# Four tail stages per chunk in place of three in the short blocks of a sparse attention kernel

## The chip, the cores and the metric

The kernel runs on one core of one Trainium2 chip. The metric is device time in microseconds for one launch. The time before is the median of three runs; the profile is of one further execution, whose own time is given beside it.

## What is computed

The input is a batch of 8 graphs with 2048 nodes and 128 features each, all with the same adjacency matrix, in which a node has some 16 neighbours on average (each entry is set with a chance of 0.0078). Four layers follow one another. Layers 0 and 1 are masked attention with 8 heads of 16, a residual, a normalisation, a feed-forward part of width 256 and a second normalisation; layers 2 and 3 are graph attention with a residual and a normalisation:

```
# layers 0 and 1
scores = einsum(Q, K) / sqrt(16);  scores = where(adj == 0, -inf, scores)
x = layer_norm(h + (softmax(scores) @ V) @ Wo + bo)
x = layer_norm(x + relu(x @ W1 + b1) @ W2 + b2)
# layers 2 and 3
h = x @ W;  e = leaky_relu(h @ a_src [i] + h @ a_dst [j]), masked by adj
x = layer_norm(softmax(e) @ h + x)
```

## The kernel before

The kernel works on the neighbours alone. It sorts the nodes by their number of neighbours and cuts them into 16 blocks of 128 (one node per partition). Block t has CAPS[t] neighbour slots: 29, 23, 21, 20, 19, 18, 17, 17, 16, 15, 15, 14, 13, 13, 12, 10. For every layer a table in memory holds one row per node (keys and values of all 8 graphs in layers 0 and 1, 8 KB), and a slot is filled by a GpSimd gather of 128 rows (`gather`, issued at L321).

A **chunk** is two slots in layers 0 and 1 and four in layers 2 and 3, so a block of 16 or 15 slots has eight chunks, one of 14 or 13 has seven, one of 12 six and one of 10 five. In `attention_chunk` VectorE multiplies keys by queries (L657) and adds halves (L663); TensorE turns the result by eight transposes and so sums it to scores (L335 into `pair`), to which masks are added (L672); ScalarE takes the exponential (L679); TensorE turns it back (L683); ScalarE copies it out as the weights (L687); VectorE multiplies the values by them (L695); TensorE sums values into `acc` by sixteen transposes (L335 into `acc`, in two halves). At the end of a block, and once in between when it has seven chunks or more, `block_sums` adds up the weights (L636, L641, L646).

When a block's last chunk is weighed, `sums` adds the two halves of the sum (L708), `scales` makes the reciprocal and turns it (L710, L730, L335 into `m`, L741), and `tail` (the function of this name) waits four slots, scales the result (`outputs`, L723) and starts the two halves of `attention_tail`, one slot and four slots later. A half tail covers four of the eight graphs: residual and Wo (L754, L759, L763), normalisation (L502, L492, L493, L509), transposes (L342), scaling (L513), two W1 products (L776) with ReLU (L781), the W2 group (L788, L793), the second normalisation, transposes, and the projection to the next layer's rows (L539, with copies L545 or L549). Each `yield` in it ends a **stage**; there are about sixteen in a half. When both halves are through, `state_done` sends the rows to the next layer's table (`put_rows`, L526).

The order of all this is written out by the kernel itself: `layers` goes over all chunks of all layers and, three times per chunk, calls `slot`. A slot advances every generator in `threads` by one step and every one in `tails` by one stage, and issues gathers (`fetch`) up to four chunks ahead, in seven buffers. It advances the tails a second time where the current chunk's layer still waits for the table of the layer before, and, in every third slot, where `hurry()` is true. `hurry()` is true only for chunks of layers 2 and 3. The engines then take their instructions in that order. Within a chunk, the second slot stands behind the scores, and the third behind the first half of the sum of the chunk two before.

The first two blocks of layers 1 to 3 can begin before the table is whole: their lists are sorted so that early slots need only the rows of earlier blocks; the rest waits for the last rows.

Of the kernel before, what the change touches and what calls it, by code (L numbers as in the profile page):

```python
# [33 lines left out]
RING = 9  # L34
STATES = 4
SCALED = 1

# [2 lines left out]
CAPS = [BASE + FOLD, 23, 21, 20, 19, 18, 17, 17, 16, 15, 15, 14, 13, 13, 12, 10]  # L42
# [47 lines left out]
def sparse_path(ctx: ExitStack, tc: tile.TileContext, ins: dict, out: bass.AP, flag: bass.AP):  # L90
# [718 lines left out]
    def gat_chunk(l, c):  # L809
# [18 lines left out]
        if c["folded"]:  # L828
            box["wf"] = small.tile([P, FOLD, NB], F32, tag="wf", name="wf", bufs=1)
            nc.vector.tensor_max(box["wf"], wa, wb)  # L830
        ws = small.tile([P, 4, SCALED], F32, tag="ws", name="ws", bufs=3)
        nc.vector.tensor_max(  # L832
            ws[:, :ns, :], wa[:, :, NB - SCALED :], wb[:, :, NB - SCALED :]
        )
        yield
        hv = hs[:, :, : NB * D].rearrange("p s (b c) -> p s b c", b=NB)
        nv = NB - SCALED
        nc.vector.tensor_mul(  # L838
# [330 lines left out]
    for l in range(4):  # L1169
        per = 2 if l < 2 else 4  # L1170
        for t, k, ns, folded in pieces(l, per):
            c = dict(l=l, t=t, k=k, ns=ns, folded=folded, box=blocks[l][t])
# [33 lines left out]
    def hurry():  # L1206

        c = every[min(now[0], len(every) - 1)]
        return c["l"] == 2 and c["t"] == NT - 1 or c["l"] > 1 and put[c["l"]] < NT

    def slot():
        advance(threads)
        advance(tails)
        fetch()
        beat[0] += 1
        c = every[min(now[0], len(every) - 1)]
        if c["l"] > 0 and put[c["l"]] < NT or beat[0] % 3 == 0 and hurry():
            advance(tails)
# [642 lines left out]
```

## Time and profile before

| what | value |
|---|---|
| median of three runs | 2790.73 us (2790.14 to 2792.69) |
| the profiled execution | 2798.62 us, of which its span 2796.7 |
| mean granted TensorE clock | 0.939 |
| block ends in layer 0 (L708), blocks 7, 13 and 15 | 681.0, 969.8, 1041.2 us |
| block ends in layer 1 (L708), blocks 7, 13 and 15 | 1556.7, 1821.9, 1887.4 us |
| last table write (L526) for layer 1, for layer 2 | 1104.3, 1949.3 us |

All times within the profile count from the span's start. Engines are named PE (TensorE products), PEld (its weight loads), DVE (VectorE), ACT (ScalarE), POOL (GpSimd) and SP (SyncE). A line of the profile's groups gives the kernel's line, the engine and operation, what is written and read, how often, the busy time and the mean length of one in ns, and then the engine's idle time just before these instructions with what ended it. A line of the timeline gives start, length, engine, line and, in brackets, the idle time before it.

### The profile page before, as it was taken

To read this page: it belongs to the slowest core of one execution; us is meant where nothing else is said; L and a number is where in the kernel's file an instruction comes from. 1 tells how busy PE (TensorE), PEld (TensorE's weight loads), DVE (VectorE), ACT (ScalarE), POOL (GpSimd) and SP (SyncE) were. 2 spreads that over 40 slices of the span, in tenths; PEclk is the share of its full clock that TensorE was granted. 3 is DMA by queue.
4 is the path that set the end of the run, shared out by engine and by line. 5 is a ranking of instruction groups with operands and counts; after the bars stand their busy time and mean duration, and the time that the engine had idled before them with its cause. 6 is when DMAs were issued, how large, how long until landed. Compare 5 with 4: busy or idle time off the path is not lost.

```text
span 2796.7 us, 48901 instructions
## 1 busy us (share of the span) xinstructions
PE 2345.7 (84%) x17811; PEld 2126.5 (76%) x17811; DVE 2513.7 (90%) x2467; ACT 1381.6 (49%) x5032; POOL 1755.3 (63%) x1346
## 2 busy tenths in 40 slices
PE   5866889898899998798989999997677887878885
PEld 4655788787788887688878888886567776878885
DVE  9698999999899897999999999986889997799995
ACT  3611444454455665154445556566346566355554
POOL 3367788678656454545565566562776776677772
PEclk9978999999999999999999999999789888999997
DMA  9898999999999888789999999984999998999994
GB/s 365 275 373 311 369 349 345 376 338 350 369 337 355 336 320 315 306 320 369 348 390 369 354 374 368 349 328 172 367 412 413 375 367 326 347 411 413 406 402 157
DMA packets 195426, 973.64 MB, mean 348 GB/s; under 512 B 30012, under 2 KB 31804, under 8 KB 123184
## 3 DMA queue, kind: packets, MB, share of 16 engines
q0 software_dynamic: 172080, 885.06, 82.5%
q1 hardware_dynamic: 18346, 60.00, 5.5%
q10 hardware_dynamic: 4752, 25.36, 2.7%
q8 instruction: 144, 2.36, 0.3%
q14 instruction: 104, 0.85, 0.1%
HBM read 917.09 MB, written 87.36 MB: 359 GB/s over the span
## 4 chain that ended last, share of the span: by engine, by line
PE 42%; DVE 24%; DMA 16%; issue 8%; ACT 8%; POOL 1%; ACTq 0%; POOLq 0%; DVEq 0%; SPq 0%
PE acc L335 15%; DMA kv<-table,lists 9%; DVE kv L695 8%; DVE kv L657 8%; PE pair L335 4%; PE m L793 4%; PE m L776 3%; PE m L539 3%; PE m L342 2%; DVE kv L838 2%; PE m L788 2%; PE m L593 2%; PE m L759 2%; PE m L763 2%; DMA table<-rows,perm 2%
## 5 line engine op out<-in xcount | busy, mean ns | idle before, releaser
L321 POOL DMA_INDIRECT kv<-table,lists x938 | 1282.2, 1367 | 678.0 <-PE acc L335 269.8
L335 PE MATMUL acc<-ident,kv 128*128 128x128 f32 x8048 | 1052.9, 285 | 159.6 <-DVE kv L695 87.9
L335 PEld LDWEIGHTS acc<-ident,kv 128*128 128x128 f32 x8048 | 957.6, 148 | 222.4 <-DVE kv L695 111.1
L695 DVE TENSOR_TENSOR kv<-kv,weights 128x2048 f32<-128x2048 f32 (+1 forms) x282 | 625.8, 2219 | 25.9 <-ACT weights L687 25.8
L657 DVE TENSOR_TENSOR kv<-kv,q 128x2048 f32<-128x2048 f32 (+1 forms) x280 | 618.2, 2208 | 32.0 <-DMA kv<-table,lists 26.3
L838 DVE TENSOR_TENSOR kv<-kv,pair 128x3584 f32<-128x3584 f32 (+1 forms) x150 | 530.8, 3538 | 1.0
L335 PE MATMUL pair<-ident,kv 128*128 128x128 f32 (+1 forms) x2256 | 301.3, 277 | 86.1 <-issue 72.8
L663 DVE TENSOR_TENSOR kv<-kv 128x1024 f32<-128x1024 f32 (+1 forms) x282 | 334.8, 1187 | 9.2
L335 PEld LDWEIGHTS pair<-ident,kv 128*128 128x128 f32 (+1 forms) x2256 | 257.0, 141 | 106.4 <-issue 85.1
L321 POOL DMA_INDIRECT kv<-table,sorted_lists x150 | 192.8, 1286 | 139.7 <-PE acc L335 42.9
L679 ACT ACTIVATE ring<-pair 128x128 f32<-128x128 f32 (+1 forms) x282 | 77.8, 276 | 365.0 <-PE pair L335 292.9
L502 ACT ACTIVATE n<-m,eps 128x128 f32<-128x128 f32 x512 | 181.5, 371 | 137.6 <-PE m L793 133.3
L687 ACT COPY weights<-pair 128x128 f32<-128x128 f32 (+1 forms) x282 | 73.3, 260 | 350.9 <-PE pair L683 342.7
L843 ACT ACTIVATE kv<-kv,ws 128x128 f32<-128x128 f32 x544 | 174.5, 398 | 145.0 <-DVE ws L832 136.4
L793 PE MATMUL m<-w_L,hT 128*128 128x128 f32 x1024 | 157.3, 276 | 0.0
L509 ACT ACTIVATE n<-m,rs 128x128 f32<-128x128 f32 x512 | 146.4, 376 | 0.3
L793 PEld LDWEIGHTS m<-w_L,hT 128*128 128x128 f32 x1024 | 136.1, 193 | 0.0
L776 PE MATMUL m<-n1T,w_L 128*128 128x512 f32 x256 | 132.9, 604 | 3.0 <-ACT hT L781 1.8
L723 DVE TENSOR_TENSOR o<-acc,scale 128x512 f32<-128x512 f32 x128 | 83.3, 684 | 52.0 <-ACT scale L741 27.1
L526 POOL DMA_INDIRECT table<-rows,perm x57 | 82.1, 1441 | 70.1 <-ACT own L562 18.7
L342 PE MATMUL m<-ident,n 128*128 128x128 f32 x640 | 114.9, 293 | 11.9 <-ACT n L509 5.6
L342 PEld LDWEIGHTS m<-ident,n 128*128 128x128 f32 x640 | 79.6, 145 | 51.0 <-ACT n L509 23.3
(254 smaller groups left out, 3614.2 us busy)
## 6 DMA issues: line engine op xcount, KB each, us to landing
kept<-xT SPq DMA_DIRECT2D x40, 512.0 KB, 6.7
kv<-in_adj_dram SPq DMA_DIRECT2D x16, 1024.0 KB, 15.6
table<-kv ACTq DMA_DIRECT2D x16, 1024.0 KB, 4.5
xT<-kept SPq DMA_DIRECT2D x32, 512.0 KB, 8.0
kv<-table,lists POOLq DMA_INDIRECT x938, 8.6
kv<-in_x_nodes_dram ACTq DMA_DIRECT2D x16, 512.0 KB, 9.9
kv<-table,sorted_lists POOLq DMA_INDIRECT x150, 6.9
home<-kept SPq DMA_DIRECT2D x4, 512.0 KB, 15.3
```

What stands on the lines that cost most here:

```text
L321: this = nc.gpsimd.indirect_dma_start(out=dst, out_offset=None, in_=tables[l][:, :] if need == NT else views[l][0], in_offset=bass.Indirec ...
L335: nc.tensor.matmul(dst, src, ident, start=start, stop=True, is_transpose=True, skip_group_check=True)
L342: nc.tensor.transpose(pt[:, j * P : (j + 1) * P], src[:, j, :], ident)
L502: nc.scalar.activation(dst[:, i, :], z[:, i, :], AF.Square, bias=eps, scale=D**-0.5, accum_out=ss[:, i : i + 1],)
L509: nc.scalar.mul(dst[:, i, :], z[:, i, :], rs[:, i : i + 1])
L657: nc.vector.tensor_mul(kk, kk, q[:, None].to_broadcast([P, ns, NB, D]))
L663: nc.vector.tensor_add(hk.rearrange("p j (c h) -> p c j h", h=NH), kj[:, :, :NH, :], kj[:, :, NH:, :])
L695: nc.vector.tensor_mul(vv, vv, w.rearrange("p (s b h) -> p (s b) h", b=NB, h=NH)[:, :, None, :] .to_broadcast([P, ns * NB, HD, NH]),)
L776: nc.tensor.matmul(ph, wt["1"][:, f * P : (f + 1) * P], n1T.rearrange("p b c -> p (b c)"), start=True, stop=True,)
L793: nc.tensor.matmul(y[:, j, :], hT[:, f, j, :], wt["2"][:, f, :], start=False, stop=f == 1, skip_group_check=True,)
L838: nc.vector.tensor_mul(hv[:, :, :nv, :], hv[:, :, :nv, :], wc[:, :, :nv, None].to_broadcast([P, ns, nv, D]))
L843: nc.scalar.mul(hv[:, i, b, :], hv[:, i, b, :], ws[:, i, b - nv : b - nv + 1])
```

## The change

A constant is added, and `hurry()` answers for layers 0 and 1 too: it is true when the current chunk belongs to a block of at most sixteen slots, that is to blocks 8 to 15. In those, one slot in three advances the tails by two stages. The chunks themselves, `threads` and the gathers keep their places.

```diff
+SHORT = 16
...
     def hurry():
         c = every[min(now[0], len(every) - 1)]
+        if c["l"] < 2:
+            return CAPS[c["t"]] <= SHORT
         return c["l"] == 2 and c["t"] == NT - 1 or c["l"] > 1 and put[c["l"]] < NT

     def slot():
         advance(threads)
         advance(tails)
         fetch()
         beat[0] += 1
         c = every[min(now[0], len(every) - 1)]
         if c["l"] > 0 and put[c["l"]] < NT or beat[0] % 3 == 0 and hurry():
             advance(tails)
```

## The prediction

> **What bounds the kernel now.** I read the page first: no engine is at its limit over the whole span, VectorE comes nearest, and TensorE follows.
>
> ```profile
> PE 2345.7 (84%) x17811; PEld 2126.5 (76%) x17811; DVE 2513.7 (90%) x2467; ACT 1381.6 (49%) x5032; POOL 1755.3 (63%) x1346
> ...
> PE 42%; DVE 24%; DMA 16%; issue 8%; ACT 8%; POOL 1%; ACTq 0%; POOLq 0%; DVEq 0%; SPq 0%
> ```
>
> The second line is the chain that ended last: TensorE holds 42% of it, VectorE 24%. An average hides the stages, so I asked for the busy time of the four stretches that the edit can touch: layer 0's blocks from the end of 8, the turn from layer 0 to 1, layer 1's blocks from 9, and the turn to layer 2. The columns are length, then busy time of PE, PEld, DVE, ACT and POOL, the clock, the DMA share and GB/s.
>
> ```profile
> 739.00:1041.00 302.00, 288.05 (x2219) 258.00 (x2218) 277.73 (x206) 171.47 (x584) 168.78 (x106) 0.98 0.91 347
> 1041.00:1105.00 64.00, 58.75 (x418) 49.31 (x417) 44.01 (x27) 41.72 (x144) 24.96 (x16) 1.00 0.76 276
> 1605.00:1887.00 282.00, 268.65 (x2169) 242.73 (x2168) 263.70 (x160) 163.77 (x623) 171.66 (x104) 0.99 0.93 354
> 1887.00:1970.00 83.00, 57.96 (x413) 49.66 (x412) 47.30 (x50) 47.50 (x174) 28.42 (x28) 0.89 0.57 197
> ```
>
> In the short blocks three resources are within reach of the bound together: TensorE 95%, VectorE 92 to 94%, DMA 91 to 93%. So what one engine does at the wrong moment is paid by another. Next, VectorE's groups in the third stretch, with its waits:
>
> ```profile
> L695 DVE TENSOR_TENSOR kv<-kv,weights 128x2048 f32<-128x2048 f32 (+1 forms) x48 | 105.9, 2208 | 4.5 <-ACT weights L687 4.5
> L657 DVE TENSOR_TENSOR kv<-kv,q 128x2048 f32<-128x2048 f32 (+1 forms) x46 | 100.7, 2189 | 0.0
> L663 DVE TENSOR_TENSOR kv<-kv 128x1024 f32<-128x1024 f32 (+1 forms) x46 | 54.3, 1180 | 1.6
> L723 DVE TENSOR_TENSOR o<-acc,scale 128x512 f32<-128x512 f32 x14 | 9.4, 687 | 4.0 <-ACT scale L741 3.5
> L708 DVE TENSOR_TENSOR block_sum<-partial 128x64 f32<-128x64 f32 x6 | 1.4, 228 | 5.3 <-ACT partial L646 5.3
> ```
>
> No chunk waits for its gather (L657: 0.0). VectorE needs 2.2 + 2.2 + 1.2 = 5.6 us per full chunk, and waits only for three things that TensorE and ScalarE make: weights, partial sums, scales. One block's heaviest part, VectorE and then TensorE:
>
> ```profile
> 1637.78 0.69 DVE L663 TENSOR_TENSOR kv<-kv 128x512 f32<-128x512 f32 x1
> 1638.39 2.28 DVE L695 TENSOR_TENSOR kv<-kv,weights 128x2048 f32<-128x2048 f32 x1
> ...
> 1644.47 2.29 DVE L695 TENSOR_TENSOR kv<-kv,weights 128x2048 f32<-128x2048 f32 x1 [0.34 <-ACT weights L687]
> ...
> 1652.57 0.22 DVE L708 TENSOR_TENSOR block_sum<-partial 128x64 f32<-128x64 f32 x1 [2.35 <-ACT partial L646]
> ```
>
> ```profile
> 1643.87 0.27 PE L683 MATMUL pair<-ident,ring 128*128 128x128 f32 x1
> ...
> 1645.78 1.04 PE L335 MATMUL pair<-ident,kv 128*64 128x128 f32 x8
> ...
> 1651.06 0.27 PE L683 MATMUL pair<-ident,ring 64*128 64x64 f32 x1
> ```
>
> The half chunk's L663 ended at 1638.5, but TensorE began its score transposes at 1645.8: it was 7.3 us behind, because tail work stands ahead of them. VectorE has two chunks (about 11.2 us) between a chunk's L663 and its L695, and in this block TensorE already uses that up: VectorE stands 0.34 + 2.35 us.
>
> [...] the 64-wide turn back (L683) had its exponentials at 1647.3 and started at 1651.06, after the tail's products ahead of it. [...] Here the tail is what is interleaved with the chunks, and the edit makes that interleaving denser and shorter.
>
> **The change part by part.** No operation is added or removed. The two instruction orders say what moves: VectorE's and SyncE's orders are the same; only TensorE's, ScalarE's and GpSimd's differ, from the block of index 8 on in layers 0 and 1. In every chunk there the third of three slots now advances the tails twice.
>
> Prices, start to start from the timeline: eight transposes 0.87 us, so a chunk (scores, two halves of the sum, one turn back) 2.73; residual and Wo products of a half tail 2.2; four transposes 0.44; one W1 product 0.86; the W2 group 2.68; a projection pair 0.45 in layer 1 (0.9 in layer 0); q 1.8; partial sums 0.7.
>
> *Full blocks of eight chunks.* Per chunk, from the one in which the first half's residual lies behind, TensorE carried (us) 5.2, 4.9, 8.9, 6.8, 4.7, 3.6, 3.6, 4.9, and now 6.2, 8.4, 8.1, 5.4, 3.3, 2.7, 3.6, 4.9. The sum is the same, but the first four go from 25.8 to 28.1, against 4 x 5.6 = 22.4 for VectorE. TensorE's order for these four, where SC is the scores and each line begins with a turn back (numbers: products of W1 or projection pairs):
>
> ```
> before  acc SC acc tr z | acc SC W1 acc W1 tr | acc q SC q y W1 acc W1 | sums acc SC tr y acc
> after   acc SC tr z acc W1 | acc W1 tr SC acc y 2xW1 | acc q SC q tr y acc proj | sums acc proj tr SC acc 2xproj
> ```
>
> I put the new order through the block above, from the turn back at 1624.2, each item at the later of its engine's turn and its input: in the second chunk the scores start at 1633.1 in place of 1631.0 and the next ones at 1641.2 in place of 1636.8, because a W2 group (2.68) and two W1 products (1.72) have come ahead of them; the third start at 1650.2, not 1645.8. The next turns back come at 1630.9, 1639.4, 1647.6, 1653.5, where they came at 1630.1, 1634.9, 1643.9, 1651.1. ScalarE's order delays the copies more: the third weight copy now stands behind a whole normalisation (squares, roots, scaling: 3.0 us) and lands at 1649.5, where VectorE wants it after L663 at 1645.9. VectorE then waits 1.8 us for the second copy and 3.4 us for the third, 5.2; the partial sums (1654.8) no longer hold it. Against 2.7 that is +2.4 us. For layer 0 the projections are dearer, but the scales stand behind no row copies any more (0.9 us of a wait of 1.2): +2.0. Three blocks each (8, 9, 10): 3 x 2.4 + 3 x 2.0 = 13.2.
>
> *Blocks of seven chunks* (11, 12, 13). There q falls into the same chunk: its TensorE work goes from 6.8 to 10.3. The same walk gives waits of 1.8 (weights), 3.7 (partial sums) and 0.3 (scales), 5.8, in place of 0.7 + 2.1 + 0.7 = 3.5: +2.2 in layer 1. In layer 0 the wait for scales falls from 2.0 to 0.6: +1.5. Sum 3 x 2.2 + 3 x 1.5 = 11.1.
>
> *Blocks of six and five* (14, 15): TensorE is the bound, its total doesn't change, and adjacent dependent stages cost short gaps: +2 in all.
>
> *The turns.* Before layer 1, all of block 14's tail stands ahead of block 15's scales in both orders (the wait of 9.9 us at 1067), so only TensorE's gaps there, 2.4 us, can go: -2. Before layer 2 block 14's tail is one stage further when block 15's begins: one W1 product (1.5 us there) and a scaling of 1.1: -3.
>
> *GpSimd and DMA.* The table writes (L526, 1.0 us each) go one or two chunks earlier past two to four gathers; nobody needs them before the next layer. Buffers come free up to 3.4 us later at the peak, and the gathers for four chunks on with them: about 12.7 us remain from release to use, against two issues (about 2.6) and a landing of 9.1: I take 0, and keep up to +2 per block.
>
> Sum: 13.2 + 11.1 + 2 - 5 = +21.3. The profiled execution took 2798.6 us (span 2796.7 and 1.9 around it): 2820. It lies 7.9 us above the median of the runs, 2790.7, so the forecast is 2812. If each of the twelve full blocks costs between 0.8 and 3.3 us, this case spans 2798 to 2830.
>
> **Rivals.** *Faster:* the tail is over before the block ends, so nothing stands before the weights and scales of the last chunks, and the heavy chunks stay inside the two chunks of slack. Then the waits for weights (5.0 us in the layer 0 stretch, 4.5 in layer 1's) go, and half of those for scales (10.6 and 3.5): -9.5 - 7 - 5 for the turns = about 2770. For it: those waits do stand behind a tail's second half. Against it: the weight copies are late now in the blocks where TensorE carries 7 us per chunk, and it gets 8 to 10. It decides if the copies come less than 11.2 us after their L663.
>
> *No change:* the lag is taken up by the light chunks before VectorE sees it; +5 in the blocks, -5 at the turns: 2791. For it: totals are equal. Against it: the block above has no slack left (0.34).
>
> *Much slower:* late releases also make gathers late, at 2 us per full block: +24 more, 2836. Against it: L657 never waits now. That the change doesn't do what it says is excluded by the two orders.
>
> **Chances.** My case 0.57, much slower 0.05, no change 0.15, faster 0.23. About 0.2% (5.6 us) is what a measurement of this kernel can tell from no change, so faster 0.23, same 0.15, slower 0.62. For 8 in 10 the range has to reach into the faster case: 2781 leaves out about 0.13 below, 2830 about 0.06 above; my case alone is 2798 to 2830.
>
> **What would show it.** Right: in 1605 to 1887 the idle time before L695, put down to the weights, grows from 4.5 to some 15 us; L657 still waits for nothing; waits for scales in layer 0 fall from 10.6 to about 4; from the L708 of block 7 to that of block 13 it takes 288.8 us in layer 0 (681.0 to 969.8) and 265.2 in layer 1 (1556.7 to 1821.9), and they grow by about 10 and 14; from the last L708 (1887.4) to layer 1's last table write (1949.3) it takes 61.9, and 3 less. Wrong: the weights' wait falls, or L657 begins to wait for gathers, or the turns shrink by over 10 us.

## The result, and the profile after

| | before | after |
|---|---|---|
| median of six runs, us | 2790.43 (2788.0 to 2800.37) | 2831.22 (2830.02 to 2832.36) |
| ratio of the runs | | 1.0143, interval 1.013 to 1.0156 |
| span of the profiled execution, us | 2796.7 | 2828.4 |
| mean granted TensorE clock | 0.939 | 0.939 |
| layer 0, end of block 7 to end of block 13 (L708), us | 288.8 | 301.0 |
| layer 1, end of block 7 to end of block 13, us | 265.2 | 291.6 |

The kernel became slower by 40.8 us; 21.3 were forecast, and 2830 was the upper end of the range. The two profiled spans differ by less, 31.7 us: the profiled execution of the kernel before lies 7.9 us above the median that the prediction started from. Lines after the added constant are numbered one higher in the kernel after (L696 is L695 of before), and two more are added below `hurry`.

The engines have the same to do; the prediction shows this line for the kernel before. From part 1 of the page of after:

```profile
PE 2344.7 (83%) x17811; PEld 2127.4 (75%) x17811; DVE 2514.1 (89%) x2467; ACT 1383.0 (49%) x5032; POOL 1787.2 (63%) x1346
```

The busy times are equal within 2 us, but for GpSimd, whose gathers take longer (the 938 that read `lists` at L321: 1367 ns on average before, 1405 after); so the loss is waiting. Three of the four stretches again, with the same work as their counterparts of before (end of block 8 to end of block 15 in layer 0, the same in layer 1, and the turn to layer 2; same columns):

```profile
730.40:1049.60 319.20, 288.96 (x2223) 258.21 (x2222) 277.30 (x206) 174.67 (x597) 186.78 (x108) 0.98 0.87 330
1613.00:1920.50 307.50, 272.55 (x2161) 245.37 (x2160) 263.92 (x160) 165.76 (x624) 187.63 (x104) 0.98 0.87 325
1921.00:2004.00 83.00, 58.45 (x416) 51.21 (x413) 49.74 (x50) 44.09 (x160) 30.56 (x29) 0.88 0.58 206
```

302 us became 319.2, and 282 became 307.5, while VectorE's busy time stayed (277.7 and 277.3, 263.7 and 263.9). The DMA share fell from 0.93 to 0.87 in layer 1, because the same bytes now take longer (354 GB/s before, 325 after). The chain of waits on the page of after can't be set beside that of before: it is followed back only to 2426 us.

VectorE's groups in layer 1 from the end of block 8 to the end of block 15, in after:

```profile
L696 DVE TENSOR_TENSOR kv<-kv,weights 128x2048 f32<-128x2048 f32 (+1 forms) x48 | 105.7, 2204 | 19.6 <-ACT weights L688 19.6
L658 DVE TENSOR_TENSOR kv<-kv,q 128x2048 f32<-128x2048 f32 (+1 forms) x46 | 100.8, 2191 | 7.5 <-ACT q L599 7.5
L664 DVE TENSOR_TENSOR kv<-kv 128x1024 f32<-128x1024 f32 (+1 forms) x46 | 54.2, 1179 | 1.6
L724 DVE TENSOR_TENSOR o<-acc,scale 128x512 f32<-128x512 f32 x14 | 9.0, 683 | 1.6 <-ACT scale L742 1.6
L709 DVE TENSOR_TENSOR block_sum<-partial 128x64 f32<-128x64 f32 x6 | 1.3, 224 | 8.8 <-ACT partial L647 8.8
```

The wait for weights rose from 4.5 to 19.6; that was forecast ("some 15"). The second line is new: the first product of a chunk waits 7.5 us for q, and none of it for gathers. The waits for partial sums grew from 5.3 to 8.8, though those in blocks of eight chunks went, as forecast: blocks 11 to 14 have 1.9 to 2.3 each, where they had 0 to 0.8.

The same groups from the end of block 7 to the end of block 13 of layer 1, before (1556.7 to 1822.0) and then after (1561.1 to 1852.8):

```profile
L695 DVE TENSOR_TENSOR kv<-kv,weights 128x2048 f32<-128x2048 f32 (+1 forms) x45 | 99.1, 2202 | 2.4 <-ACT weights L687 2.4
L657 DVE TENSOR_TENSOR kv<-kv,q 128x2048 f32<-128x2048 f32 (+1 forms) x45 | 98.4, 2187 | 0.0
...
L723 DVE TENSOR_TENSOR o<-acc,scale 128x512 f32<-128x512 f32 x12 | 7.9, 685 | 1.6 <-ACT scale L741 1.3
L708 DVE TENSOR_TENSOR block_sum<-partial 128x64 f32<-128x64 f32 x7 | 1.6, 232 | 7.4 <-ACT partial L646 7.4
```

```profile
L696 DVE TENSOR_TENSOR kv<-kv,weights 128x2048 f32<-128x2048 f32 (+1 forms) x45 | 98.9, 2197 | 21.6 <-ACT weights L688 21.6
L658 DVE TENSOR_TENSOR kv<-kv,q 128x2048 f32<-128x2048 f32 (+1 forms) x45 | 98.5, 2189 | 8.7 <-ACT q L599 8.7
...
L724 DVE TENSOR_TENSOR o<-acc,scale 128x512 f32<-128x512 f32 x12 | 7.7, 682 | 0.0
L709 DVE TENSOR_TENSOR block_sum<-partial 128x64 f32<-128x64 f32 x7 | 1.6, 226 | 6.9 <-ACT partial L647 6.9
```

These waits are the loss of this stretch: together they grow from 11.1 to 37.2 us, by 26.1, and the time grew by 26.4. Weights have 19.2 of it and q 8.7; scales and partial sums give 1.8 back.

One block of eight chunks, layer 1's block 9, VectorE, then TensorE, then two lines of ScalarE, in after:

```profile
1645.76 0.69 DVE L664 TENSOR_TENSOR kv<-kv 128x512 f32<-128x512 f32 x1
1649.32 2.29 DVE L696 TENSOR_TENSOR kv<-kv,weights 128x2048 f32<-128x2048 f32 x1 [2.86 <-ACT weights L688]
1652.78 2.29 DVE L658 TENSOR_TENSOR kv<-kv,q 128x2048 f32<-128x2048 f32 x1 [1.16 <-ACT q L599]
...
1658.60 2.29 DVE L696 TENSOR_TENSOR kv<-kv,weights 128x2048 f32<-128x2048 f32 x1 [2.27 <-ACT weights L688]
```

```profile
1641.95 1.04 PE L336 MATMUL pair<-ident,kv 128*128 128x128 f32 x8
1642.82 1.04 PE L336 MATMUL acc<-ident,kv 128*128 128x128 f32 x8
1643.69 0.39 PE L789 MATMUL m<-center,n1T 128*128 128x128 f32 x2
...
1646.37 1.88 PE L777 MATMUL m<-n1T,w_L 128*128 128x512 f32 x4
1648.09 0.27 PE L684 MATMUL pair<-ident,ring 128*128 128x128 f32 x1
```

```profile
1655.26 0.37 ACT L503 ACTIVATE n<-m,eps 128x128 f32<-128x128 f32 x1 [1.85 <-PE m L794]
...
1658.29 0.28 ACT L688 COPY weights<-pair 128x128 f32<-128x128 f32 x1
```

The first wait is read across the first two. The scores began at 1641.95, but their L664 had ended at about 1636.7: TensorE was 5.2 us behind. Then a half sum, a W2 group (2.68) and both W1 products of the other half (1.72) stood ahead of the turn back at 1648.09. Its copy was there at 1649.3, and VectorE, ready at 1646.4, had stood 2.86 us. The last wait stands behind a normalisation on ScalarE: the turn back of that chunk ran on TensorE at 1656.38, but the copy only at 1658.29, for the second half's squares, which had themselves waited for TensorE, began at 1655.26.

### The profile page after: what moved, and what is told of

It is laid out like the page before. It is cut to its first block, busy times and chain, and to the rows that moved or that the text cites. A ratio compares the mean times of both kernels' runs of the same rounds, so it can differ in the third digit from the quotient of the medians.

```text
span 2828.4 us, 48889 instructions
## 1 busy us (share of the span) xinstructions
PE 2344.7 (83%) x17811; PEld 2127.4 (75%) x17811; DVE 2514.1 (89%) x2467; ACT 1383.0 (49%) x5032; POOL 1787.2 (63%) x1346
## 5 line engine op out<-in xcount | busy, mean ns | idle before, releaser
L322 POOL DMA_INDIRECT kv<-table,lists x938 | 1317.6, 1405 | 682.4 <-PE acc L336 362.4
L696 DVE TENSOR_TENSOR kv<-kv,weights 128x2048 f32<-128x2048 f32 (+1 forms) x282 | 625.8, 2219 | 61.8 <-ACT weights L688 61.8
L658 DVE TENSOR_TENSOR kv<-kv,q 128x2048 f32<-128x2048 f32 (+1 forms) x280 | 618.3, 2208 | 34.9 <-ACT q L599 17.2
L664 DVE TENSOR_TENSOR kv<-kv 128x1024 f32<-128x1024 f32 (+1 forms) x282 | 334.8, 1187 | 9.2
L343 PE MATMUL m<-ident,n 128*128 128x128 f32 x640 | 111.3, 289 | 12.5 <-ACT n L510 6.4
L343 PEld LDWEIGHTS m<-ident,n 128*128 128x128 f32 x640 | 78.9, 144 | 48.9 <-ACT n L510 22.4
## 6 DMA issues: line engine op xcount, KB each, us to landing
kv<-in_x_nodes_dram ACTq DMA_DIRECT2D x16, 512.0 KB, 10.3
```

What stands on the lines that cost most here:

```text
L322: this = nc.gpsimd.indirect_dma_start(out=dst, out_offset=None, in_=tables[l][:, :] if need == NT else views[l][0], in_offset=bass.Indirec ...
L343: nc.tensor.transpose(pt[:, j * P : (j + 1) * P], src[:, j, :], ident)
L658: nc.vector.tensor_mul(kk, kk, q[:, None].to_broadcast([P, ns, NB, D]))
L664: nc.vector.tensor_add(hk.rearrange("p j (c h) -> p c j h", h=NH), kj[:, :, :NH, :], kj[:, :, NH:, :])
L696: nc.vector.tensor_mul(vv, vv, w.rearrange("p (s b h) -> p (s b) h", b=NB, h=NH)[:, :, None, :] .to_broadcast([P, ns * NB, HD, NH]),)
```

## The experiments

The kernels ran on several chips, whose times for the kernel before differ (2791 to 2911 us). A ratio is always to the kernel before on the same chip, or, within a pair, the quotient of two such ratios. Beside it I give the length of layer 1 from the end of block 7 to the end of block 13 ("the stretch"; 265.2 us before, 291.6 after, +26.4), which depends less on the chip: the profile of a run shows it directly. Two runs below in which layer 1's blocks 8 to 13 are as before give 265.5 (`l0_only`) and 264.0 (`short12`), so a profile repeats it within about 1 us.

### Where the loss lies

Two kernels take the change in one layer alone; `l1_only` asks for layer 1.

```diff
-            return CAPS[c["t"]] <= SHORT
+            return c["l"] == 0 and CAPS[c["t"]] <= SHORT
```

> The double stage in layer 0 alone. Read from the trace of the changed kernel, layer 0 and the turn behind it cost about 10 us (its clock stands at -5.5 us at the end of block 7 and at +4.5 at the last table write), so both theories expect about 2800 us, ratio 1.0035. If the loss were one effect of both layers together, the two halves would not add up to 41 us.

> The double stage in layer 1 alone. From the trace layer 1 and the turn to layer 2 cost 27 us (from +4.5 to +31.8), so about 2818 us, ratio 1.0098, and with the layer 0 kernel a sum near 41 us.

Measured: 1.0048 (1.0029 to 1.0066) and 1.0102 (1.0064 to 1.014). Together that is 1.5%, so the layers add up, and layer 1 carries two thirds. The stretch of `l1_only` has the length of after's, 291.6.

A third kernel sets `SHORT = 12`: only blocks 14 and 15 have four stages.

> The double stage only in the blocks of 12 and 10 slots (14 and 15), where a tail is longer than the block, and so at the turns. From the steps between block ends in the changed kernel's trace: layer 0 -0.5 + 2.2 - 4.0, layer 1 -1.2 + 4.0 - 1.8, together about -1 us: ratio 0.999 to 1.002. If the turns gain what the prediction put there (5 us) and the blocks cost 2, 0.999.

Measured: 1.0021 (1.0006 to 1.0037), slightly above what was expected: blocks 14 and 15 took 2 to 4 us more each, and the turn to layer 1 was 3.9 shorter. So nearly all of the loss lies in blocks 8 to 13.

### Is it the place of the double stage, or the two halves together?

`half` doubles every sixth slot. `phase1` doubles the first of three slots, in layers 2 and 3 too, so only its stretch is a clean comparison. In `apart9` the second half of a tail starts nine slots after `tail` releases it in place of four, so eight slots after the first half in place of three.

```diff
-            return CAPS[c["t"]] <= SHORT
+            return beat[0] % 6 == 0 and CAPS[c["t"]] <= SHORT
```

> The second stage is given only in every sixth slot of the short blocks: three and a half stages per chunk. Lag theory (what counts is how far TensorE's summed work runs ahead of VectorE's 5.6 us per chunk at its peak): in a block of eight chunks the peak is 5.5 us, against 5.9 with four stages and 3.4 with three, worked out from the order with the prices of the prediction; so four fifths of the loss stay, ratio about 1.012. Doubling theory (each slot that holds two dependent stages of a tail costs by itself): half as many doubled slots, half the loss, about 1.007.

```diff
-        if c["l"] > 0 and put[c["l"]] < NT or beat[0] % 3 == 0 and hurry():
+        if c["l"] > 0 and put[c["l"]] < NT or beat[0] % 3 == 1 and hurry():
```

> Four stages per chunk, but the doubled slot is the first of a chunk's three, ahead of its scores, and not the third. Lag theory: peak 5.5 us, ratio about 1.012. Place theory (the loss comes from the double slot standing ahead of the copy of the weights): the copy is free of it, the scores are late instead; 1.005 or less if the place is the cause.

```diff
-            tails.append(later(4, lambda: attention_tail(l, t, box, 4)))
+            gap = 9 if CAPS[min(t + 1, NT - 1)] <= 16 else 4
+            tails.append(later(gap, lambda: attention_tail(l, t, box, 4)))
```

> Four stages per chunk as changed, but in the short blocks the second half of a tail starts nine slots after it is released and not four, so its heavy products no longer fall into the chunks of the first half's. The number of doubled slots grows, if anything. Lag theory: the peak is 4.4 us (before 3.4, changed 5.9), so two fifths of the loss stay, ratio about 1.006. Doubling theory: the loss stays, 1.014 or more.

Measured: 1.0168 (1.0148 to 1.0189), 1.0154 (1.0134 to 1.0174) and 1.0269 (1.0244 to 1.0294); stretches 289.8, 292.5, 289.8. Half as many double slots cost as much as all, so it isn't the doubled slot by itself, and its place in the chunk makes no difference. `apart9` refuted a figure of mine: I had summed TensorE's work per chunk and expected two fifths of the loss with the halves apart. Its stretch is as long as after's (its larger ratio comes from elsewhere, the turn to layer 1 among it, 5.7 us longer). TensorE's scores wait there 17.0 us for ScalarE's copies of the weights:

```profile
L336 PE MATMUL pair<-ident,kv 128*128 128x128 f32 (+1 forms) x360 | 47.7, 275 | 18.4 <-ACT weights L688 17.0 <-issue 1.4
```

In the same stretch of before that wait was 0.5, in after 7.4. The scores and the turned weights share the tile `pair` (here and below such a tile is called a bank), the scores in columns 0 to 127, the turned weights from 128 on. Though these don't overlap, the traces show the next scores standing until ScalarE has copied the weights before them, as for 1.24 us at 1634.57 in after; why they must isn't shown. My walk had left it out.

### Is it that bank?

Two ways to take the wait away, each with three and with four stages. In the first, a chunk's turn back and copy are written out ahead of the third slot's stages (not where partial sums are formed).

```diff
             for c2 in weighed[-1:]:
-                go(c2)
+                if not c2.pop("early", False):
+                    go(c2)
...
+            if c["l"] in (0, 1) and CAPS[c["t"]] <= SHORT and not c["last"] and not c["leave"] and len(c["box"]["exps"]) < RING - 2:
+                c["early"] = True
+                go(c)
             slot()
```

> Three stages as before, with the same early turn back and copy in the short blocks. Crowding theory: no gain, 2788 to 2795 us. Place theory: the waits of VectorE for weights in the short blocks, 5.0 us in layer 0 and 4.5 in layer 1, go at least in part, 2780 to 2787 us.

> Four stages per chunk as changed, but in the short blocks a chunk's turn back and its weight copy are written ahead of the third slot's tail stages and no longer behind them (the chunks that form partial sums excepted). Crowding theory (what costs is that TensorE's tail work falls into four chunks in place of six): the crowding is the same, so the loss stays, 2820 us or more. Place theory (what costs is that ScalarE's copy of the weights stands behind a normalisation of 1.9 us, and that the next chunk's scores wait for that copy because both use the PSUM tile pair): most of the loss goes, 2800 us or less, and TensorE's wait of 1.24 us for the copy disappears.

In the second, the turn back goes to one of the three rotating banks.

```diff
-        back = pair[:, P : P + m]
+        back = misc()[:, :m]
```

> The kernel before, with each chunk's exponentials turned back into a bank of the three that rotate, not into the bank that holds the scores: so the next scores don't wait for ScalarE's copy of the weights. Three stages per chunk. In the kernel before TensorE waits for that 0.5 us in all in blocks 8 to 13 of layer 1, so both theories expect 0.995 to 1.003; the rotation may bring waits for banks of its own.

> The same bank for the turn back, with four stages per chunk. TensorE's waits of the scores for the weights' copy were 7.4 us (layer 1) and 6.2 (layer 0) with four stages. Bank theory: without them the loss falls to at most a third: ratio to the kernel with three stages and this bank at most 1.005. Slack theory: what counts is that the tail work stands ahead of the copies, bank or no bank: ratio at least 1.010.

Measured: early 1.0141 (1.0105 to 1.0177) and 1.0272 (1.0229 to 1.0316), back 1.009 (1.0051 to 1.013) and 1.0353 (1.0298 to 1.0407). Four stages against three cost 1.0129 and 1.0261 (intervals of about 0.006 and 0.007 to either side). The stretches grow by 20.3 (278.3 to 298.6) and 45.7 (266.5 to 312.2). The wait for the bank (7.4 us in after) is gone in both; the loss isn't. But neither way is clean. Both cost time with three stages already, which I had not expected: with the early copy VectorE waits 13.6 us for scales in blocks 12 and 13 alone. And with four stages other waits take the place of the one that went: VectorE waits 27.0 us for q with the early copy; with the other bank, TensorE's partial sums and turns back wait 10.7 and 5.6 us for banks that ScalarE has yet to read. So taking the wait for the bank away brought nothing back, and it isn't shown to be the cause.

### Does more slack help?

In blocks 8 to 13 the product with the weights comes three chunks, not two, after the sum of products. Seven buffers allow it only with gathers three chunks ahead.

```diff
-            if len(weighed) > 2:
+            while len(weighed) > (3 if held(i) else 2):
...
+            if held(now[0]) or held(now[0] - 1):
+                if now[1] - now[0] > 3:
+                    return
```

(`held` is true for chunks of blocks 8 to 13 of layers 0 and 1. There is a fourth buffer for the weights, and one ring row fewer.)

> The kernel before, with three chunks of slack in place of two between a chunk's sum of products and the product with its weights, in blocks 8 to 13 of layers 0 and 1 (so one chunk more is held back; a fourth buffer for weights, one ring row fewer, gathers three chunks ahead in place of four there). Three stages per chunk. The lag of the copied weights behind the sum of products is at most 14.0 us in the kernel before, and three chunks are 16.8. Slack theory: the waits for weights (2.4 in layer 1, 2.9 in layer 0, us) go, those for scales and partial sums stay or move: ratio to before 0.995 to 1.000. Bank theory (the scores wait for ScalarE's copy of the turned weights, since both lie in one bank): ratio 1.000, since nothing changes in what TensorE waits for. If the gathers, three chunks ahead, come late, L657 begins to wait and the ratio rises over 1.002; then only the difference to the kernel with four stages counts.

> The same slack of three chunks, with four stages per chunk. The lag is at most 19.4 us and over 16.8 in few chunks. Slack theory: the loss is that the lag passes what VectorE has, so it nearly goes: ratio to the kernel with three stages and three chunks of slack at most 1.005. Bank theory: TensorE itself stands while it waits for the copies, so the loss stays: ratio at least 1.010.

Measured: 1.0068 (1.0048 to 1.0088) and 1.0341 (1.0292 to 1.0389), a quotient of 1.0271; the stretch 279.6 and 311.0. The slack theory missed. The bank theory's figure (at least 1.010) came, but not shown to be for its reason. VectorE's first two groups in the stretch of `slack_four`:

```profile
L696 DVE TENSOR_TENSOR kv<-kv,weights 128x2048 f32<-128x2048 f32 (+1 forms) x45 | 98.7, 2195 | 0.0
L658 DVE TENSOR_TENSOR kv<-kv,q 128x2048 f32<-128x2048 f32 (+1 forms) x44 | 96.4, 2192 | 58.7 <-DMA kv<-table,lists 37.9 <-ACT q L599 10.1 <-PE m L642 6.9
```

The weights no longer end a wait. But each buffer is held a chunk longer, and the gathers come late: 37.9 us (16.1 with three stages). The slack was only moved from one side of the seven buffers to the other. Slack without that price, with an eighth buffer, was not measured.

### Which engine's work makes the copies late?

`fewer` leaves out half of the sum in blocks 8 to 13, 0.87 us of TensorE's work in a full chunk.

```diff
-            add_up(acc, kv[:, i : i + 1, :, D:], k + i, 1, c["folded"])
+            if i == 0 or not 8 <= t <= 13:
+                add_up(acc, kv[:, i : i + 1, :, D:], k + i, 1, c["folded"])
```

> The kernel before, but in blocks 8 to 13 of layers 0 and 1 TensorE adds up only the first slot of each chunk: half of the sum, 0.87 us of TensorE's work per chunk, is left out, all else stays. Three stages per chunk; what counts is the difference to the next kernel. It was 26.4 us in layer 1's blocks 8 to 13 and 15.7 in layer 0's blocks 9 to 13 between the kernels before and after. Expected here: VectorE's waits for weights and partial sums go, 0.99 to 1.00 of before.

> The same half sum left out, with four stages per chunk. TensorE has 39 us less to do in layer 1's blocks 8 to 13. If the loss is that TensorE's work of the heavy chunks passes what VectorE's slack covers, it falls to at most 8 us in layer 1's blocks 8 to 13, and the ratio to the kernel with three stages to at most 1.005. If it is the chain of hand-overs between TensorE and ScalarE that no idle TensorE shortens, it stays at 18 us or more there, ratio 1.010 or more.

`plain` leaves out squares and roots of the normalisations that run beside these blocks, and scales by a constant in one instruction in place of four.

```diff
+        if 7 <= t <= 12:
+            yield
+            nc.scalar.mul(dst, z, 0.5)
+            yield
+            return
```

> The kernel before, but the tails of blocks 7 to 12 in layers 0 and 1 (which run beside blocks 8 to 13) leave out the squares and roots of their two normalisations: ScalarE multiplies by 0.5 in one instruction where it had four squares, two for the roots and four scalings (3.0 us). TensorE and VectorE have the same to do. Three stages per chunk; expected 0.99 to 1.00 of before, since weights, sums and scales stand behind less.

> The same short normalisations with four stages per chunk. If the loss is that the copies of the weights stand behind the squares and roots on ScalarE, so that both VectorE and TensorE's next scores wait, it falls to at most 8 us in layer 1's blocks 8 to 13, ratio to the kernel with three stages at most 1.005. If TensorE's load of the heavy chunks makes the loss, it stays at 18 us or more, ratio 1.010 or more.

`free` lets TensorE's products inside these tails read the identity, so that none of TensorE's stages needs ScalarE's answer to the stage ahead. TensorE still waits for banks, and ScalarE still for TensorE.

```diff
-        pt = transpose4(n1)
+        pt = transpose4(same if free else n1)
...
-                y[:, j, :], n1T[:, j, :], center, start=j == 0, stop=False,
+                y[:, j, :], ident if free else n1T[:, j, :], center, start=j == 0, stop=False,
```

(and so for W1, W2, the second transposes and the projection.)

> The kernel before, but in the tails of blocks 7 to 12 of layers 0 and 1 TensorE's transposes and the products with W1, W2, the center and the projection read the identity, not what ScalarE made in the stage ahead of them. Every instruction of every engine stays; left out is only that TensorE waits for ScalarE's answer inside a tail (it still waits for a bank whose content three products ago ScalarE hasn't copied). Three stages per chunk; what counts is the difference to the next kernel. Expected 0.99 to 1.00 of before.

> The same cut with four stages per chunk. Chain theory: the loss is that stages of one tail that need each other follow each other with less chunk work between, so TensorE stands for ScalarE's answers and the partial sums and weights behind it come late; without that need the loss falls to at most 10 us in layer 1's blocks 8 to 13 (26.4 between the kernels before and after) and the ratio to the kernel with three stages to at most 1.007. Order theory: the loss is that TensorE's and ScalarE's queues have more in front of the weights' copies, need or no need; then it stays at 18 us or more there, ratio 1.010 or more.

| pair | ratio to before, three stages | four stages | quotient | stretch, us |
|---|---|---|---|---|
| the change itself | 1 | 1.0143 | 1.0143 | 265.2 to 291.6, +26.4 |
| `fewer` | 0.9979 (0.997 to 0.9988) | 1.0218 (1.0196 to 1.024) | 1.0240 | 263.7 to 299.3, +35.6 |
| `plain` | 0.9999 (0.999 to 1.0007) | 1.0107 (1.009 to 1.0124) | 1.0108 | 261.0 to 281.0, +20.0 |
| `free` | 0.999 (0.9974 to 1.0006) | 1.0145 (1.0124 to 1.0165) | 1.0155 | 262.8 to 295.2, +32.4 |

A quotient's interval is 0.002 to 0.003 to either side. `free` shows that TensorE's need of ScalarE's answers isn't the cause. `plain` takes a quarter of the loss away, 6.4 of 26.4 us; by its expectation (18 us or more) that still leaves most of it to TensorE. `fewer` came out against my theory: with less for TensorE to do the loss grew. It isn't a clean test, though. In its stretch TensorE's clock fell (column before the last two: 0.95 with three stages, 0.93 with four; 0.98 and 0.97 before and after):

```profile
1541.60:1805.30 263.70, 229.40 (x1667) 196.03 (x1666) 252.39 (x154) 146.04 (x561) 153.59 (x93) 0.95 0.95 369
```

```profile
1577.00:1876.30 299.30, 237.77 (x1697) 206.51 (x1696) 253.12 (x154) 154.63 (x581) 145.57 (x93) 0.93 0.85 327
```

Summed over slices of 2 us, length times one less the clock, that is 12.0 and 22.2 us of full-clock time (5.1 before, 8.5 after). Even if these 10 us all lay on the path, 25 would be left. The other two pairs aren't even in this either: `plain` goes from 3.4 to 11.9 and `free` from 3.4 to 13.7. If all of that lay on the path, `free` would grow by 22 us without it and the change itself by 23, so what `free` says stands. `plain` would grow by 11.5, so the normalisations' part lies between a quarter and a half. That the clock isn't the cause of the loss is shown by `apart9`: it loses 5.1 us to the clock, as before, and its stretch is 24.6 us longer.

### What the traces say of the lag

From the timelines I took, for each of the 45 chunks of the stretch, the time from the end of L663 to the end of the weights' copy, and summed what exceeds VectorE's 11.2 us.

| kernel | mean lag, us | largest | sum over 11.2 | stretch | VectorE waits for weights, for q |
|---|---|---|---|---|---|
| before | 9.2 | 14.0 | 13 | 265.2 | 2.4, 0 |
| `plain_three`, `free_three`, `fewer_three` | 8.8, 8.9, 9.3 | 12.5, 13.4, 13.6 | 5, 10, 10 | 261.0, 262.8, 263.7 | 1.2 to 2.6, 0 |
| `plain_four` | 10.3 | 16.4 | 49 | 281.0 | 10.2, 8.0 |
| `apart9` | 11.4 | 18.0 | 65 | 289.8 | 16.9, 2.8 |
| `early_four` | 10.0 | 19.8 | 66 | 298.6 | 7.6, 27.0 |
| `half` | 11.1 | 18.6 | 74 | 289.8 | 7.1, 15.3 |
| `phase1` | 11.0 | 17.7 | 75 | 292.5 | 8.9, 17.9 |
| after | 11.3 | 19.4 | 80 | 291.6 | 21.6, 8.7 |
| `free_four`, `fewer_four` | 11.4, 11.7 | 19.4, 21.0 | 86, 99 | 295.2, 299.3 | 22.6 and 26.0, 11.1 and 11.7 |
| `back_four` | 12.7 | 21.4 | 128 | 312.2 | 29.9, 12.0 |

But for `early_four` the order of the sums is nearly that of the stretches. (`early_three`, whose stretch of 278.3 is long for its waits for scales, isn't in the table: its sum is about 15.) It is a sign of the loss and no account of it, for a chunk that has stood for q needs its weights later: in `half` and `phase1` q ends most of the waits, and the loss is the same. Whoever looks at the weights alone would think those two cured.

Split by its parts, the mean lag of after against before grows by 1.53 us from L663 to the end of the exponential (5.35 to 6.88), by 0.13 from there to the turn back, and by 0.49 from the turn back to the copy (0.82 to 1.31). So seven tenths of the growth come before the exponential is through, and 0.49 in ScalarE's queue ahead of the copy; in `plain` that last part doesn't grow (0.71 and 0.64).

The first part can be split once more. From L663's end to the start of TensorE's scores it is 3.75 us before and 5.38 after; from there to the end of the exponential nothing is added (1.49 and 1.40). Summed over the 45 chunks, an instruction counted for every chunk that it keeps waiting, TensorE works for 165 us of these intervals before and for 226 after, and stands for 4 and 17 (7.4 of that for the bank). The tails' products have 70 of the work before and 100 after, the products for q 5 and 15. So the scores are late mostly because more of the tail and of q stands ahead of them in TensorE's order. That is read from the traces; no run takes it away by itself.

ScalarE's groups show the turn of that queue. Before:

```profile
L687 ACT COPY weights<-pair 128x128 f32<-128x128 f32 (+1 forms) x45 | 11.6, 258 | 53.6 <-PE pair L683 52.7
```

After:

```profile
L503 ACT ACTIVATE n<-m,eps 128x128 f32<-128x128 f32 x96 | 33.9, 365 | 70.8 <-PE m L764 44.6 <-PE m L794 26.2
...
L688 ACT COPY weights<-pair 128x128 f32<-128x128 f32 (+1 forms) x45 | 11.6, 259 | 4.9 <-PE pair L684 4.5
```

Before, ScalarE stood ready for the weights 53.6 us in all. Now it stands 44.6 us at the squares of the residual (L764), whose products TensorE hasn't made, with the copy behind; when it comes to the copy, the turn back is mostly done (4.9). This is a sign of the crowding rather than its cause: in `phase1` ScalarE stands only 7.3 us at those squares, and the loss is the same.

The chain of waits of `l1_only`, whose layer 1 goes as after's does, can be added up for the stretch: of 291.6 us ScalarE holds 36.0 (15.0 of 265.2 before), TensorE 150.0 (163.9), and gathers, absent before, 18.5. No wait of VectorE's in the groups above is put down to them yet, but they have come within reach.

## Why the prediction was wrong, step by step

- **The place and the kind of the loss: right.** Blocks 8 to 13, VectorE standing for weights, L657 (L658 of after) waiting for no gather there, the turn to layer 2 1.8 shorter (forecast 3), to layer 1 4.0 (forecast 2). Waits for scales in layer 0's stretch fell from 10.6 to 4.4 (forecast: about 4). Blocks 14 and 15 cost 1.7 in layer 0 and 2.8 in layer 1, where +2 stood for both.
- **Layer 0: some three tenths too small.** The terms gave 6.0 + 4.5 + 1 - 2 = 9.5; alone it cost 0.48% (`l0_only`), 13.4 us of 2790. Blocks 9 to 13 cost +4.8, +3.7, +1.6, +3.2 and +2.3, where +2.0 and +1.5 stood. (Block 8 came out 3.4 shorter, but 3.7 shorter also where layer 0 is untouched, in `l1_only`: the profiled execution of before waited 3.6 us for gathers and 4.5 for a list there, `l1_only` 1.2 and 3.3. So the 288.8 us of before are long: layer 0's blocks 8 to 13, untouched, take 282.1 in `l1_only` and 282.5 in `short12`, and the change costs more there than the 12.2 us of the first table.)
- **Layer 1: the miss.** The terms gave 7.2 + 6.6 + 1 - 3 = 11.8; alone it cost 1.02%, 28.5 us.
- **The waits that the kernel before has in these blocks: the step that failed first.** For layer 1 the sum sets its waits after the change against 2.7 us in each block of eight chunks and 3.5 in each block of seven, 18.6 in six blocks. The kernel before waits 11.1 there: 2.1, 2.7 and 1.4, then 0, 1.3 and 3.6. Only the block walked and the last block had what I put for all. Where TensorE still had room, the whole of the new wait is loss. That is 7.5 of the 12.6 us by which the stretch grew more than forecast (26.4, not 13.8). I had walked one block and carried its waits over to the others, though the groups' sum of before could have told it.
- **The waits after: the smaller miss.** 33.0 us were forecast, 37.2 measured: 5.5, 6.3 and 6.3 in blocks of eight chunks (forecast 5.2), 4.8, 7.9 and 6.5 in blocks of seven (5.8). So the blocks cost +3.6, +3.7 and +5.0, where +2.4 stood, and +5.0, +6.4 and +2.7, where +2.2 stood. (The differences written there are also a tenth low: 5.2 less 2.7 is 2.5, 5.8 less 3.5 is 2.3.)
- **The walk through block 9: right in kind, and nearly in size.** The block shown comes 8.0 us later than the one walked. With that taken off, the scores start 0.8 to 1.2 us after the times of the walk, in its order. The wait for the second copy was put at 1.8 and is 2.86. That for the third, behind a whole normalisation, was put at 3.4 and is 1.16 for q and then 2.27. Partial sums no longer end a wait (2.35 before), as forecast. The walk had left out that scores wait for the copy in the same bank (1.24 us at 1634.57), and it put VectorE's wait for q, whose copy (L599) stands behind the tail's products, at nothing without a reason. In this block q only takes a part of the wait for the third copy; in blocks 12 and 13 it adds 2.8 and 2.1, where the forecast had more for partial sums (3.7; measured 2.3).
- **Load as the reason: seen in the traces, not shown by a run.** I set 28.1 us of TensorE's work against 22.4 of VectorE's. `apart9` and `fewer` didn't follow that count: in `apart9` TensorE stands for the bank instead (ahead of the scores it works for 212 us and stands for 34, after 226 and 17), in `fewer` the clock fell. What grows is the lag in two queues, three quarters of it ahead of the scores, where TensorE is at work on more of the tail and of q. How much of the loss would go if only that work went, the runs don't settle; a run of `fewer` at an even TensorE clock would tell.
- **The rivals.** "Faster" stood on copies that come less than 11.2 us after their L663; 20 of 45 came later, 9 before. "Much slower" named gathers; they end no wait in after's layer 1, but they are next: given a chunk more of slack, they took it.

## What to carry to other kernels

Side work that is interleaved with a stream can cost by its spacing alone: moving it closer together left every engine's work as it was and still cost 1.4%. The chunks that it left lighter gave little back, as I read it because VectorE hardly waited in them before. Measure, per item, how late a result comes against the slack that its reader has, in every stretch and not in one, and price the new lag against the waits that are there now, block by block. When a wait goes away on one engine, look at once for the next reader: here it went from partial sums to weights in blocks of eight chunks, with the early copy from the bank to q, and with more slack from weights to gathers.

## What the runs showed of the hardware

TensorE runs at half rate early in two of the six blocks 8 to 13 of layer 1 before, and in four of them after. In the first of these VectorE is busy 99% of the time, TensorE stands for it, and its clock falls. Stretches of 4 us of the kernel before, and TensorE in them:

```profile
1564.00:1568.00 4.00, 2.78 (x26) 2.57 (x25) 3.96 (x4) 1.39 (x4) 3.39 (x3) 1.00 1.02 426
1568.00:1572.00 4.00, 1.71 (x10) 1.47 (x9) 4.00 (x3) 0.28 (x1) 3.39 (x3) 0.64 1.00 415
1572.00:1576.00 4.00, 4.00 (x20) 3.85 (x19) 3.96 (x3) 0.00 (x0) 2.70 (x2) 0.51 1.04 429
1576.00:1580.00 4.00, 3.95 (x32) 3.36 (x31) 3.96 (x4) 3.29 (x16) 2.14 (x2) 1.00 1.01 420
```

```profile
1570.70 1.97 PE L335 MATMUL acc<-ident,kv 128*128 128x128 f32 x8 [2.29 <-DVE kv L695]
1572.46 0.63 PE L754 MATMUL m<-parts_z,ones_bf 128*128 128x512 bf16 x1
1572.89 0.64 PE L759 MATMUL m<-center,xT 128*128 128x128 f32 x2
...
1580.23 0.38 PE L759 MATMUL m<-center,xT 128*128 128x128 f32 x2
1580.46 0.39 PE L763 MATMUL m<-w_L,o 128*128 128x128 f32 x2
```

The residual products of the first half start 0.43 us apart, those of the second, 8 us later, 0.22. My prices were those of the second. In slices of 0.25 us the granted clock of this stretch is 1.00 or 0.50, but for the slices in which it changes: it stands at 0.50 for 6.8 us from 1569.1 on and for 3.4 us from 1620.3 on, and in after for 6.8 us once and for 3.4 us three times. Each of these six spells begins during a wait of TensorE for L695 (L696 of after) of 2.29 us, or within 1.2 us of its end. Such a wait doesn't always bring one: in after, waits of 1.17 and then 2.29 us, with eight transposes between them, end at 1728.86, and the clock stays at 1.00, where 1.22 and 2.29 went with the spell shown. So what takes the clock down isn't shown. The spells cost 5.1 us of the stretch before and 8.5 after, so they are a part of the loss, at most 3.4 of 26.4. The lost time comes in steps of about 1.7 us (1.7, 3.4, 5.1, 8.5, 11.9, 13.7 and 22.2 in the stretches of the runs), which is what a spell of 3.4 us at 0.50 costs. With half of the sum left out of TensorE's work it is larger, 12.0 in `fewer_three` against 5.1; that may be why `fewer_three` gained only 1.5 us in the stretch, which isn't shown.
